# A graph network's node products, each block's transpose moved between the second and third product of the block before

## The chip, the core and the metric

The kernel runs on one core of one Trainium2 chip. The metric is the device time of one execution in microseconds (us); lower is better. Five engines work side by side on the core[...]: TensorE (PE: matrix products and transposes), VectorE (DVE: elementwise work, sums, statistics), ScalarE (ACT: activations and copies), GpSimd (POOL: here mainly the issue of gathers) and SyncE (SP: the issue of other transfers). PEld in the profile is TensorE's loading of a stationary operand.

## The reference

Two layers of a graph network on 10,000 nodes of 512 features, with 160,000 edges in order of their target. The first layer, cut to what matters:

```python
h = relu(layernorm(x))
h_all = einsum('nd,rdf->nrf', h, rel_W) + rel_b      # four products per node
agg = segment_mean(h_all[src, edge_type], dst)       # gathered over the edges
h1 = h @ self_W + self_b + agg                       # a fifth product per node
x1 = layer_norm(h + h1)
x = x + layer_norm(x1 + gelu(x1 @ W1 + b1) @ W2 + b2)
```

The second layer gathers and sums rows twice more, with two products per node each time. The change concerns only the first two lines and `h @ self_W`: the five 512x512 products of every node, called the node stage here.

## The kernel before

The nodes are taken in blocks of 128 (78 full blocks and one of 16 nodes), and the blocks in groups of four. For each block the node stage normalizes the rows, turns them on TensorE (a transpose is a product with the identity; four of them for 512 columns), copies the result out of PSUM with ScalarE, and multiplies it by five weights. All is float32, and each product of 128x512 shows as two instructions in the trace, so five products with four slabs of 128 each are 40 matmul instructions per block.

```python
def transposed(psum, dest, rows, r):
    p = psum.tile([P, KC, P], F32, name="pT")
    for k in range(KC):                                   # KC = 4
        nc.tensor.transpose(p[:, k, :r], rows[:, k * P:(k + 1) * P], ident[:r, :r])
    nc.scalar.copy(dest, p[:, :, :r])

def products(g):
    b0, nb, r = g
    xg = loaded.pop()
    sc = norm_scales(ap_, [xg[:r, c, :] for c in range(nb)], r, "a")
    hg = xp.tile([P, 4, D], F32, name="hg")
    for c in range(nb):
        h = hg[:r, c, :]
        nc.scalar.activation(h, xg[:r, c, :], AF.Relu, bias=sc[c][1], scale=sc[c][0])
        hT = ap_.tile([P, KC, P], F32, name="hT")
        transposed(psT, hT[:, :, :r], h, r)
        nc.vector.tensor_tensor(h, h, bself[:r], op=OP.add)
        nc.vector.tensor_tensor(xg[:r, c, :], xg[:r, c, :], ln2b[:r], op=OP.add)
        ha = ap_.tile([P, R, D], F32, name="ha")
        for j, w in enumerate([wself] + wrel):            # five products
            pm = psM.tile([P, D], F32, name="pm")
            for k in range(KC):
                nc.tensor.matmul(pm[:r], hT[:, k, :r], w[:, k, :], start=(k == 0),
                                 stop=(k == KC - 1))
            ...                                           # VectorE adds the bias out of PSUM
        nc.scalar.dma_start(hall_d[n0:n0 + r, :], ha[:r].rearrange("p r d -> p (r d)"))
        ...
        next(step, None)                                  # one step of the edge lists
    nc.sync.dma_start(rows_of(xs_d, g), hg[:r, :nb])
    nc.sync.dma_start(rows_of(xr_d, g), xg[:r, :nb])

for g, later in zip(groups, groups[1:] + [None]):
    products(g)
    if later:
        load(later)
```

The pools: `hT`, `ha`, `hg` and `xg` have two buffers each, the transpose's `pT` one bank of PSUM, the products' `pm` four banks, and the edge lists three banks.

`next(step)` carries on a second piece of work in small portions: the lists that say which rows each node gathers. They are worked out mostly on VectorE, with small products on TensorE in between: `pe<-inl,inb` (192 instructions), `pe<-win,of` (393) and `pe<-kept,beyond` (156). The order of the instructions on each engine in this stage is made by the scheduler of the language, which takes, in program order, what is ready by its own account of time; so an instruction may be issued before one that stands ahead of it in the text, but an engine then works through its queue in that fixed order.

Behind the node stage stands a branch that needs its results (whether the lists fit), and behind the branch the gathers and all that follows, in an order that is written by hand.

Of the kernel before, what the change touches and what calls it, by code (L numbers as in the profile page):

```python
# [8 lines left out]
F32 = mybir.dt.float32  # L9
# [3 lines left out]
AF = mybir.ActivationFunctionType  # L13
# [3 lines left out]
P = 128  # L17
# [4 lines left out]
def kernel(  # L22
# [33 lines left out]
    nc = tc.nc  # L56
    N, D = x.shape
# [3 lines left out]
    KC = D // P  # L61
# [10 lines left out]
    groups = [(b, min(4, full - b), P) for b in range(0, full, 4)]  # L72
# [59 lines left out]
    def rows_of(t, g):  # L132

        b, nb, r = g
        return t[b * P:b * P + nb * r, :].rearrange("(c p) d -> p c d", p=r)

    def wide(pool, row, n, name):

        t = pool.tile([P, n], F32, name=name)
        nc.sync.dma_start(t, bass.AP(tensor=row.tensor, offset=row.offset, ap=[[0, P], [1, n]]))  # L140
        return t

    def weight(pool, w, k, n, name, queue=nc.scalar):
        t = pool.tile([P, k, n], F32, name=name)
        queue.dma_start(t, w.rearrange("(k p) n -> p k n", p=P))
        return t

    def norm_scales(pool, vals, r, name):

        nb = len(vals)  # L150
        st = pool.tile([P, nb, 6], F32, name=f"st{name}")
        mv = pool.tile([P, nb, 2], F32, name=f"mv{name}")
        rs = pool.tile([P, 2, nb], F32, name=f"rs{name}")
        for c, v in enumerate(vals):
            nc.vector.bn_stats(st[:r, c, :], v)
            nc.vector.bn_aggr(mv[:r, c, :], st[:r, c, :])
        nc.scalar.activation(rs[:r, 0, :], mv[:r, :, 1], AF.Sqrt, bias=eps[:r], scale=1.0)
        nc.vector.reciprocal(rs[:r, 0, :], rs[:r, 0, :])
        nc.vector.scalar_tensor_tensor(rs[:r, 1, :], mv[:r, :, 0], -1.0, rs[:r, 0, :],
                                       op0=OP.mult, op1=OP.mult)  # L160
        return [(rs[:r, 0, c:c + 1], rs[:r, 1, c:c + 1]) for c in range(nb)]
# [7 lines that stand above are left out]
# [400 lines left out]
    def edges(ep, ep2, pse):  # L569
        found = {k: ep.tile([P, NB], F32, name=f"f_{k}")   # L570
                 for k in ["first", "deg", "from", "upto"] + [
                     f"{k}{lv}" for lv in range(NL) for k in ("sfrom", "supto", "sbase")]}
        with ExitStack() as s:
            yield from runs(s.enter_context(tc.tile_pool(name="er", bufs=1)), ep2, pse, found)
        with ExitStack() as s:
            yield from lists(s.enter_context(tc.tile_pool(name="el", bufs=1)), ep2, pse, found)


    with ExitStack() as s:
        pse = s.enter_context(tc.tile_pool(name="pse", bufs=3, space=PSUM))  # L580
        wp = s.enter_context(tc.tile_pool(name="wp", bufs=1))
        xp = s.enter_context(tc.tile_pool(name="xp", bufs=2))
        ap_ = s.enter_context(tc.tile_pool(name="ap", bufs=2))
        psT = s.enter_context(tc.tile_pool(name="psT", bufs=1, space=PSUM))
        psM = s.enter_context(tc.tile_pool(name="psM", bufs=4, space=PSUM))

        ep = s.enter_context(tc.tile_pool(name="ep", bufs=1))
        ep2 = s.enter_context(tc.tile_pool(name="ep2", bufs=2))
        step = edges(ep, ep2, pse)
        loaded = []  # L590

        def load(g):
            b0, nb, r = g
            loaded.append(xp.tile([P, 4, D], F32, name="xg"))
            nc.sync.dma_start(loaded[-1][:r, :nb], rows_of(x, g))

        load(groups[0])
        wself = weight(wp, self_w, KC, D, "wself")
        bself = wide(wp, self_b, D, "bself")
        wrel = [weight(wp, rel_w[0], KC, D, "wrel0", nc.sync)]  # L600
        brel = wide(wp, rel_b, R * D, "brel")
        wrel += [weight(wp, rel_w[r], KC, D, f"wrel{r}", nc.sync) for r in range(1, R)]
        ln2b = wide(wp, ln2_b, D, "ln2b")

        def products(g):
            b0, nb, r = g
            xg = loaded.pop()
            sc = norm_scales(ap_, [xg[:r, c, :] for c in range(nb)], r, "a")
            hg = xp.tile([P, 4, D], F32, name="hg")
            for c in range(nb):  # L610
                h = hg[:r, c, :]
                nc.scalar.activation(h, xg[:r, c, :], AF.Relu, bias=sc[c][1], scale=sc[c][0])
                hT = ap_.tile([P, KC, P], F32, name="hT")
                transposed(psT, hT[:, :, :r], h, r)
                nc.vector.tensor_tensor(h, h, bself[:r], op=OP.add)
                nc.vector.tensor_tensor(xg[:r, c, :], xg[:r, c, :], ln2b[:r], op=OP.add)
                ha = ap_.tile([P, R, D], F32, name="ha")
                for j, w in enumerate([wself] + wrel):
                    pm = psM.tile([P, D], F32, name="pm")
                    for k in range(KC):  # L620
                        nc.tensor.matmul(pm[:r], hT[:, k, :r], w[:, k, :], start=(k == 0),  # L621
                                         stop=(k == KC - 1))
                    if j:
                        nc.vector.tensor_tensor(ha[:r, j - 1, :], pm[:r],  # L624
                                                brel[:r, (j - 1) * D:j * D], op=OP.add)
                    else:
                        nc.vector.tensor_tensor(h, pm[:r], h, op=OP.add)
                n0 = (b0 + c) * P
                nc.scalar.dma_start(hall_d[n0:n0 + r, :], ha[:r].rearrange("p r d -> p (r d)"))
                gate[:] = [ha[:, 0, :1]] if r == P else []  # L630
                if b0 + c >= 2:
                    next(step, None)
            nc.sync.dma_start(rows_of(xs_d, g), hg[:r, :nb])
            nc.sync.dma_start(rows_of(xr_d, g), xg[:r, :nb])

        for g, later in zip(groups, groups[1:] + [None]):
            products(g)
            if later:
                load(later)
        gate.clear()  # L640
        for _ in step:
            pass

    def aligned(ctxa):
# [58 lines left out]
        with ExitStack() as s:  # L703
# [209 lines left out]
            for bs in plan:  # L913
                for b in bs:
                    r = height(b)
                    if b == bs[0]:
                        before, grp = grp, Group(bs)
                    if i + 2 < len(blocks):
                        load(blocks[i + 2])
                    if i + 1 < len(blocks):  # L920
                        hot = hots(blocks[i + 1])
                    got = second()
                    pa, mine = held
                    add(b, pa, mine)
                    v = nodes[b]
                    nc.vector.scalar_tensor_tensor(v[:r], pa[:r], rdeg[:r, b:b + 1], v[:r],
                                                   op0=OP.mult, op1=OP.add)
                    first = (b, now.stats(v[:r], r))
                    part = products(queue.pop(0) if queue else [], turning)
                    next(part)  # L930
                    now.finish()
                    scaled(got, first)
                    next(part, None)
                    if i + 1 < len(blocks):
                        held = begin(blocks[i + 1], hot, table)

                    if b == bs[0] and before:
                        queue += before.parts()
                    turning = lambda g=grp, b=b, v=v: g.turn(b, v)
                    i += 1  # L940
            turning()
            queue += grp.parts()
            while queue or fed or third:
                got = second()
                part = products(queue.pop(0) if queue else [], None)
                next(part)
                now.finish()
                scaled(got, None)
                next(part, None)
# [395 lines left out]
```

## Time and profile before

| What | Value |
|---|---|
| Time, median of 3 | 6551.81 us (6546.44 to 6563.14) |
| Span of the profiled execution | 7257.0 us |
| First product of the node stage starts | 15.61 us |
| Its last products start, and last 17.35 us | 1492.65 us |
| First gather behind the branch | 1514.47 us |
| PE busy over the whole span | 5628.8 us (78%) |
| The products, L621, on four weights and on one | 1097.8 us and 297.1 us busy |
| The transposes, L167, x316 | 48.0 us busy |
| The copies out of PSUM, L168, x79 | 45.9 us busy |

A row of the timeline gives the start, the duration, the engine, the line of the kernel, the operation with output<-input and shape, the number of instructions merged into the row, and in brackets how long the engine had been idle before and what ended it. The ends of matmuls are modelled, so intervals from start to start say more of TensorE's pace than durations do. The profiled execution is longer than the timed ones; absolute times within the node stage are read from the profile.

### The profile page before, as it was taken

Reading aid. Unit: us, or ns where it says so; the run is one execution under the profiler, and the core shown is the slowest. Engines: PE = TensorE matmul, PEld = TensorE weight load, DVE = VectorE, ACT = ScalarE, POOL = GpSimd, SP = SyncE. Lnnn points to the kernel's source line nnn. Section 1 sums busy time; section 2 is a strip of 40 time slices with the busy share of each in tenths; the row PEclk is TensorE's granted clock in tenths of the full one; section 3 lists DMA queues with packets and bytes.
Section 4 is the critical chain, followed back from the end, with each engine's and each line's share of the span. In section 5 each row is a group of like instructions: output and inputs, shape, how many; then the busy total and the mean of one; then the engine's idle time right before and its main releaser. Section 6 shows DMA issues by size and latency. Waiting matters only on the chain.

```text
span 7257.0 us, 49943 instructions
## 1 busy us (share of the span) xinstructions
PE 5628.8 (78%) x14251; PEld 2540.8 (35%) x14251; DVE 3650.8 (50%) x7301; ACT 1019.6 (14%) x1667; POOL 3807.2 (52%) x3927
## 2 busy tenths in 40 slices
PE   8999999967888899888676666666666666666666
PEld 4444444423333334333333323332322232333232
DVE  6467786235666666666334333443434444444444
ACT  1000000012222333322210010101000000000000
POOL 0001110046666666665366666666656666666665
PEclk9999999988999999999888888888887888888888
DMA  4223232256777777775466667666666777776775
GB/s 168 93 105 112 95 117 88 84 178 191 215 222 223 224 231 221 213 216 182 154 206 207 204 203 210 205 205 205 205 206 209 218 210 213 221 218 213 218 223 169
DMA packets 457021, 1360.83 MB, mean 188 GB/s; under 512 B 71902, under 2 KB 71902, under 8 KB 446606
## 3 DMA queue, kind: packets, MB, share of 16 engines
q0 software_dynamic: 308768, 1008.91, 47.1%
q1 hardware_dynamic: 136174, 265.65, 10.3%
q10 hardware_dynamic: 11792, 82.97, 2.8%
q8 instruction: 114, 1.87, 0.1%
q14 instruction: 173, 1.42, 0.1%
HBM read 1150.25 MB, written 207.01 MB: 187 GB/s over the span
## 4 chain that ended last, share of the span: by engine, by line
PE 35%; issue 23%; another core or an unknown queue 17%; DVE 4%; ACT 3%; POOL 2%; DMA 1%; ACTq 0%; POOLq 0%; DVEq 0%; SPq 0%
PE pa L688 10%; PE ph L784 6%; PE pm L621 5%; PE po L795 5%; PE po L992 4%; PE po L1026 3%; DVE pa L700 2%; POOL rows L661 2%; PE pT L167 1%; ACT hTb L168 1%; ACT mTb L168 1%; ACT mb L1022 0%; DMA rows<-hall_d,row 0%; DMA rows<-h_d,row 0%
## 5 line engine op out<-in xcount | busy, mean ns | idle before, releaser
L700 DVE TENSOR_TENSOR pa<-pa,rows 128x512 f32<-128x512 f32 x2574 | 1798.5, 699 | 991.1 <-issue 676.5
L661 POOL DMA_INDIRECT rows<-h_d,row x1716 | 1668.4, 972 | 917.5 <-issue 422.8
L661 POOL DMA_INDIRECT rows<-hall_d,row x858 | 854.2, 996 | 516.7 <-issue 193.0
L688 PE MATMUL pa<-rows,hot 128*128 128x512 f32 (+1 forms) x2358 | 1082.1, 606 | 40.0 <-issue 28.0
L992 PE MATMUL po<-wns,mTb 128*128 128x512 f32 (+1 forms) x1264 | 687.2, 694 | 537.8 <-ACT mTb L168 274.5
L1026 PE MATMUL po<-wss,hTb 128*128 128x512 f32 (+1 forms) x1264 | 710.8, 715 | 507.3 <-ACT hTb L168 393.0
L621 PE MATMUL pm<-wrel,hT 128*128 128x512 f32 (+1 forms) x2528 | 1097.8, 592 | 0.0
L661 POOL DMA_INDIRECT rows<-h_d,orow x786 | 754.7, 960 | 404.3 <-issue 223.9
L784 PE MATMUL ph<-x1T,w1s 128*128 128x512 f32 (+2 forms) x1344 | 588.0, 591 | 163.0 <-issue 88.9
L621 PEld LDWEIGHTS pm<-wrel,hT 128*128 128x128 f32 (+1 forms) x2528 | 477.3, 189 | 607.6 <-issue 584.6
L688 PEld LDWEIGHTS pa<-rows,hot 128*128 128x128 f32 (+1 forms) x2358 | 454.3, 193 | 636.5 <-issue 607.8
L661 POOL DMA_INDIRECT rows<-hall_d,orow x393 | 373.2, 950 | 453.3 <-SPq L1341 327.3
L992 PEld LDWEIGHTS po<-wns,mTb 128*128 128x128 f32 (+1 forms) x1264 | 275.6, 224 | 934.5 <-issue 631.3
L795 PE MATMUL po<-w2s,hid 128*128 128x512 f32 (+1 forms) x1264 | 564.2, 598 | 33.5 <-issue 28.7
L1026 PEld LDWEIGHTS po<-wss,hTb 128*128 128x128 f32 (+1 forms) x1264 | 277.4, 231 | 888.6 <-ACT hTb L168 448.9
L688 PE MATMUL pa<-tail,hot 128*128 128x512 f32 x936 | 465.6, 615 | 69.5 <-issue 60.7
L998 DVE TENSOR_TENSOR po<-po,bss 128x512 f32<-128x512 f32 (+1 forms) x79 | 55.0, 696 | 815.9 <-remote 740.7
L494 POOL DMA_INDIRECT win<-rec_d,at x79 | 80.4, 1018 | 661.9 <-issue 568.9
L784 PEld LDWEIGHTS ph<-x1T,w1s 128*128 128x128 f32 x1344 | 258.7, 200 | 461.7 <-issue 375.1
L624 DVE TENSOR_TENSOR ha<-pm,brel 128x512 f32<-128x512 f32 (+1 forms) x316 | 217.0, 687 | 389.5 <-PE pm L621 388.9
L1002 DVE TENSOR_TENSOR ob<-po,bss 128x512 f32<-128x512 f32 (+1 forms) x79 | 54.5, 690 | 608.8 <-remote 283.1
L795 PEld LDWEIGHTS po<-w2s,hid 128*128 128x128 f32 (+1 forms) x1264 | 237.1, 190 | 318.9 <-issue 310.8
(237 smaller groups left out, 4144.6 us busy)
## 6 DMA issues: line engine op xcount, KB each, us to landing
hall_d<-ha ACTq DMA_DIRECT2D x78, 1024.0 KB
hb<-h_d SPq DMA_DIRECT2D x38, 1024.0 KB
rows<-h_d,row POOLq DMA_INDIRECT x1716
xs<-xs_d SPq DMA_DIRECT2D x39, 512.0 KB
xr<-xr_d SPq DMA_DIRECT2D x39, 512.0 KB
xn_d<-xr SPq DMA_DIRECT2D x39, 512.0 KB
h_d<-h SPq DMA_DIRECT2D x39, 512.0 KB
xg<-in_x_dram SPq DMA_DIRECT2D x19, 1024.0 KB
```

What stands on the lines that cost most here:

```text
L167: nc.tensor.transpose(p[:, k, :r], rows[:, k * P:(k + 1) * P], ident[:r, :r])
L168: nc.scalar.copy(dest, p[:, :, :r])
L494: nc.gpsimd.indirect_dma_start(out=win[:, c, :], out_offset=None, in_=rec_d, in_offset=bass.IndirectOffsetOnAxis(ap=at[:, c:c + 1], axis=0))
L621: nc.tensor.matmul(pm[:r], hT[:, k, :r], w[:, k, :], start=(k == 0), stop=(k == KC - 1))
L624: nc.vector.tensor_tensor(ha[:r, j - 1, :], pm[:r], brel[:r, (j - 1) * D:j * D], op=OP.add)
L661: nc.gpsimd.indirect_dma_start(out=t[:n], out_offset=None, in_=table, in_offset=bass.IndirectOffsetOnAxis(ap=idx, axis=0))
L688: nc.tensor.matmul(pa[:r], hot[:, t, :r], others[t], start=(t == order[0]), stop=(t == order[-1]))
L700: nc.vector.tensor_tensor(pa[:r], pa[:r], t[:r], op=OP.add)
L784: nc.tensor.matmul(ph[:, :n], w1s[:, k, f * P:(f + 1) * P], self.xT[:, k, :n], start=(k == 0), stop=(k == KC - 1))
L795: nc.tensor.matmul(po[:r], self.hid[:, f, c * r:(c + 1) * r], w2s[:, f, :], start=(f == 0), stop=(f == FC - 1))
L992: nc.tensor.matmul(po[:r], mT[:, k, :r], wns[:, k, :], start=False, stop=(k == KC - 1))
L1026: nc.tensor.matmul(po[:r], hT[:, k, :r], wss[:, k, :], start=(k == 0), stop=False)
```

## The change

The products of all groups become one run of blocks. A block's rows are no longer turned at its own beginning but in the block before it, between that block's second and third product; the scales of a group's norms are worked out at the beginning of the last block of the group before. What it is for: while ScalarE copies the transpose out of PSUM, TensorE should have products to do. Loading the next group's rows moves to the head of the group's loop in the text. The number of instructions of every kind stays the same, and so do the pools.

```diff
-        def products(g):
+        def opened(g):
             b0, nb, r = g
             xg = loaded.pop()
-            sc = norm_scales(ap_, [xg[:r, c, :] for c in range(nb)], r, "a")
-            hg = xp.tile([P, 4, D], F32, name="hg")
+            return (xg, norm_scales(ap_, [xg[:r, c, :] for c in range(nb)], r, "a"),
+                    xp.tile([P, 4, D], F32, name="hg"))
+
+        def turned(g, rows, c):
+            r = g[2]
+            xg, sc, hg = rows
+            nc.scalar.activation(hg[:r, c, :], xg[:r, c, :], AF.Relu, bias=sc[c][1],
+                                 scale=sc[c][0])
+            hT = ap_.tile([P, KC, P], F32, name="hT")
+            transposed(psT, hT[:, :, :r], hg[:r, c, :], r)
+            return hT
+
+        rows = opened(groups[0])
+        hT = turned(groups[0], rows, 0)
+        for i, g in enumerate(groups):
+            b0, nb, r = g
+            xg, _, hg = rows
+            later = groups[i + 1] if i + 1 < len(groups) else None
+            if later:
+                load(later)
             for c in range(nb):
                 h = hg[:r, c, :]
-                nc.scalar.activation(h, xg[:r, c, :], AF.Relu, bias=sc[c][1], scale=sc[c][0])
-                hT = ap_.tile([P, KC, P], F32, name="hT")
-                transposed(psT, hT[:, :, :r], h, r)
                 ...
                 for j, w in enumerate([wself] + wrel):
+                    if j == 0 and c == nb - 1 and later:
+                        rows = opened(later)
+                    if j == 2 and c < nb - 1:
+                        hT_next = turned(g, rows, c + 1)
+                    elif j == 2 and later:
+                        hT_next = turned(later, rows, 0)
                     pm = psM.tile([P, D], F32, name="pm")
                     ...
+                hT = hT_next
...
-        for g, later in zip(groups, groups[1:] + [None]):
-            products(g)
-            if later:
-                load(later)
```

## The prediction

> **What bounds the kernel now.** I began with the slices of the page, to find the node stage and what limits it.
>
> ```profile
> PE   8999999967888899888676666666666666666666
> POOL 0001110046666666665366666666656666666665
> PEclk9999999988999999999888888888887888888888
> ```
>
> A slice is 181 us. In the first eight PE is at 9 while POOL does next to nothing; then the gathers begin and PE is no longer full. So the node stage is TensorE's, at full clock, and lasts about 1,500 us. Next, what happens at its end (POOL's timeline):
>
> ```profile
> 1514.47 0.94 POOL L661 DMA_INDIRECT rows<-hall_d,orow  x1 [327.26 <-SPq L1341]
> ```
>
> GpSimd has waited 327 us at the branch. Nothing behind the branch starts before the stage is over, so what the stage loses or gains goes into the total one for one. That carries the prediction: I need only the stage's change in microseconds. The chain of waits over the stage shows which engine sets it:
>
> ```profile
> 1269.96 17.43 PE pm L621 x40
> 1287.92 0.60 ACT hT L168
> 1288.56 17.43 PE pm L621 x40
> ...
> 1492.65 17.35 PE pm L621 x40
> 1510.03 0.69 DVE ha L624
> 1510.74 2.56 DMA hall_d<-ha
> ```
>
> Block after block: 40 products, then ScalarE's copy of the next transpose, then 40 products. PE's timeline of one such block, without edge work:
>
> ```profile
> 1287.23 0.60 PE L167 MATMUL pT<-ident,hg 128*128 128x128 f32 x4
> 1288.56 3.70 PE L621 MATMUL pm<-wself,hT 128*128 128x512 f32 x8 [0.73 <-ACT hT L168]
> 1292.10 13.90 PE L621 MATMUL pm<-wrel,hT 128*128 128x512 f32 x32
> 1305.83 0.60 PE L167 MATMUL pT<-ident,hg 128*128 128x128 f32 x4
> ```
>
> Start to start: a period of 18.60 us (1287.23 to 1305.83). The four transposes and the wait for the copy take 1.33, the first eight products 3.54, the other 32 take 13.73, so 0.429 each. At that pace the first eight would take 3.43; the wait costs 0.11 more there. The same place with edge work:
>
> ```profile
> 552.19 0.60 PE L167 MATMUL pT<-ident,hg 128*128 128x128 f32 x4
> 552.63 0.53 PE L519 MATMUL pe<-win,of 128*128 128x82 bf16 x10
> 553.00 0.32 PE L548 MATMUL pe<-kept,beyond 128*128 128x82 bf16 x4
> 553.52 3.70 PE L621 MATMUL pm<-wself,hT 128*128 128x512 f32 x8 [0.21 <-ACT hT L168]
> ```
>
> The transposes take 0.44 to the next start. Then the edge products run inside the wait for the copy (0.21 idle is left of 0.73), and from 552.19 to 553.52 is again 1.33. So the small edge products are free today: they fill the very gap that the change closes.
>
> [...] the load for a transpose stands at 1286.80, before the products are through, while behind the wait two loads come bunched, which is my reading of the 0.11. [...] The gaps here are 1.33 at most in the steady run, and the granted clock reads 1.00, so closing them wins no clock. [...] Here 32 products of 592 ns each would be 18.9 us and take 13.73, so I count starts. [...]
>
> **The change part by part.**
>
> *Transposes between the second and third product.* A block now is 40 products at 0.429, 17.16 us, plus the transposes, 0.44, plus what the switch to them and back costs. The way there costs nothing visible (their start follows at the products' pace); the way back I put at 0.1 us, an estimate from the 0.11 that bunched weight loads cost above. Sum 17.70 against 18.60: 0.90 saved. There are 78 passages from one block to the next: 0.90 x 78 = 70 us.
>
> *The edge products lose their hiding place.* 393 of `pe<-win,of` and 156 of `pe<-kept,beyond`; ten of them took 0.37 from 552.63 to 553.00, 0.037 each: 549 x 0.037 = 20 us, now on TensorE's path wherever the scheduler puts them. The 192 of `pe<-inl,inb` were never hidden (a period with 32 of them, from 318.82 to 340.86, is 22.04, longer by 3.44): no change.
>
> *The second block.* It starts at 37.40 after a wait of 2.44 instead of 0.73, since the first group's start ran into ScalarE's other work. With its transpose seven microseconds into block one that goes: 1.7 us saved.
>
> *Norms a block ahead, loads at the head of the loop.* Already today the scheduler runs them early: the relus of four blocks stand together at 1222.69, and the next group starts at 1232.81. In the text they move, in time hardly. 0.
>
> *Evictions and stores.* Same number, same place; VectorE takes 0.69 per product of 3.43 and `pm` has four banks. 0.
>
> Sum: 70 + 1.7 - 20 = 52 us. I take off 7 for stalls: today two edge products waited 2.50 and 3.18 us for VectorE with the queue behind them, and smaller lateness was swallowed by the gap, which it won't be any more. 45 us remain, and the stage ends near 1465 instead of 1510: 6551.8 - 45 = 6507 us, 0.7% less.
>
> **The rivals.**
>
> *VectorE takes over in the list stretch.* For it (the window from 850 to 1000 us; columns are PE, PEld, DVE, ACT and POOL busy, granted clock, DMA share, GB/s):
>
> ```profile
> 850.00:1000.00 150.00, 145.64 (x461) 68.15 (x460) 123.41 (x535) 11.14 (x18) 16.27 (x16) 0.99 0.27 101
> ```
>
> VectorE is busy 82% here. With 70 - 20 us off some 1,480 the share rises to about 85%: still below TensorE, but more edge products would come late. The lists occupy about 750 us, some 40 blocks. If a third of those blocks met a stall of 2.5 us, that took 33 us, and the gain shrank to about 20: 6532. Against it: only two such stalls today, and they depend on the scheduler's order more than on load.
>
> *The copy is held up on ScalarE.* Its queue can stand at relus that wait for a store:
>
> ```profile
> 1222.69 2.93 ACT L612 ACTIVATE hg<-xg,rsa 128x512 f32<-128x512 f32 x4 [8.79 <-DMA xs_d<-hg]
> ```
>
> That block began at 1213.96. If the next block's copy stands behind these relus, it starts 11.7 us into the block and is done by 12.3, and is needed at 17.7. Slack of five microseconds; cost nothing. If such a pile-up came later in the block, at 20 group ends, 20 x 2 = 40 us would be lost: 6545, no change.
>
> *The edge products stay hidden.* They might fill bubbles at the switch back to products. Then 20 us come on top: gain 70, 6482. I see no gap of that size in a queue that always has products ready, so I give it little.
>
> *Nothing comes through, because the branch waits for something else.* The lists end at about 1250 us, 260 before the stage does, so only the last block's products and its store of 2.56 us stand before the gathers. Against this rival.
>
> **Range and chances.** The working gives 6507. The largest doubts are the way back from the transposes (0 to 0.25 us each, +8 to -12 us in all) and stalls of edge products (0 to 30 us); the times of before spread over 17 us. I say 6488 to 6533 for 8 in 10. Two per cent is 131 us; the waits to be had are 1.33 + 0.11 - 0.44 = 1.0 us in 78 passages, 78 us, so faster by 2% can't come from this mechanism: 0.02. Slower by 2% would need 1.7 us lost at every block, or a bad order: 0.02. Within 2%: 0.96.
>
> **What would show it.** Right: in blocks without edge work a period of about 17.7 us, with 16 products, four transposes, 24 products; the wait of PE for the copy (30.5 us in 67 cases today) gone; edge products adding some 0.5 us to a block that has them; the first gather near 1470. Wrong: idle time of PE before `pe` products with VectorE as releaser, well above 5.7 us; a bubble of over 0.25 us behind the transposes; PE waiting for the copy or for relus in mid-block; or a granted clock under 1.00 in the stage.

## The result, and the profile after

| | Before | After |
|---|---|---|
| Time, median | 6553.04 us (4 runs) | 6504.61 us (4 runs, 6497.32 to 6506.94) |
| Ratio to before | | 0.9923, 95% interval 0.9906 to 0.9940 |
| First gather behind the branch | 1514.47 us | 1461.25 us |
| PE waits for the copy, `pm <- hT` | 30.5 us, 67 times | 0.7 us, once |
| PE waits for VectorE before `pe` products | 3.2, 2.5 and 0.4 us | none |

The kernel is 48 us faster, 0.8%; run again beside other kernels it came to 6496.57 us, ratio 0.9919 (0.9906 to 0.9933). The profiled execution of the kernel before ran slower behind the branch than its timed ones, so traces are compared up to the first gather only.

The slices of the page after (40 equal parts of the span, each digit a share in tenths):

```profile
PE   9999999996999999999877777777778777777777
POOL 0001111007777777777277777777767777777776
PEclk9999999998999999999998889888888998888988
```

A slice is 163 us now; the stage fills the first nine, at a granted clock of 1.00 (the window from 20.5 to 1460.8 us). POOL's timeline at the branch:

```profile
1461.25 0.95 POOL L681 DMA_INDIRECT rows<-hall_d,orow  x1 [313.11 <-SPq L1361]
```

The gathers still wait for the stage, and begin 53.2 us earlier. The chain of waits of this profile covers only the last instructions of the execution, so what sets the stage is read from PE's timeline. A block without edge work:

```profile
1252.43 0.60 PE L167 MATMUL pT<-ident,hg 128*128 128x128 f32 x4
1252.87 10.46 PE L645 MATMUL pm<-wrel,hT 128*128 128x512 f32 x24
1263.17 3.60 PE L645 MATMUL pm<-wself,hT 128*128 128x512 f32 x8
1266.60 3.60 PE L645 MATMUL pm<-wrel,hT 128*128 128x512 f32 x8
1270.03 0.60 PE L167 MATMUL pT<-ident,hg 128*128 128x128 f32 x4
```

No brackets: nothing was waited for. Transposes to transposes is 17.60 us, against 18.60. The transposes take 0.44, and the 24 products behind them 10.30, which is 24 times the usual 0.429: coming back to products costs nothing. A block with edge work:

```profile
507.62 10.46 PE L645 MATMUL pm<-wrel,hT 128*128 128x512 f32 x24
517.92 0.53 PE L519 MATMUL pe<-win,of 128*128 128x82 bf16 x10
518.29 0.32 PE L548 MATMUL pe<-kept,beyond 128*128 128x82 bf16 x4
518.45 3.67 PE L645 MATMUL pm<-wself,hT 128*128 128x512 f32 x8
521.95 1.45 PE L645 MATMUL pm<-wrel,hT 128*128 128x512 f32 x3
```

The edge products stand between two blocks and take their full 0.53 us, and the eight products behind them 3.50 instead of 3.43. (The last row is cut off by the window of the view; the next product of the block begins at 521.95.) And the list stretch, the window from 850 to 1000 us (columns: length, then busy time of PE, PEld, DVE, ACT and POOL, granted clock, DMA share, GB/s):

```profile
850.00:1000.00 150.00, 150.00 (x478) 70.02 (x477) 123.60 (x547) 11.72 (x19) 16.43 (x16) 1.00 0.29 106
```

TensorE has no idle time at all in it; VectorE is as busy as before.

### The profile page after: what moved, and what is told of

It is laid out like the page before. It is cut to its first block, busy times and chain, and to the rows that moved or that the text cites. A ratio compares the mean times of both kernels' runs of the same rounds, so it can differ in the third digit from the quotient of the medians.

```text
span 6504.3 us, 49918 instructions
## 1 busy us (share of the span) xinstructions
PE 5603.6 (86%) x14251; PEld 2472.9 (38%) x14251; DVE 3632.4 (56%) x7301; ACT 1013.0 (16%) x1667; POOL 3823.7 (59%) x3927
## 5 line engine op out<-in xcount | busy, mean ns | idle before, releaser
L708 PE MATMUL pa<-rows,hot 128*128 128x512 f32 (+1 forms) x2358 | 1364.7, 718 | 673.8 <-DMA rows<-h_d,orow 615.9
L708 PEld LDWEIGHTS pa<-rows,hot 128*128 128x128 f32 (+1 forms) x2358 | 492.8, 225 | 1537.7 <-DMA rows<-h_d,orow 1078.5
L681 POOL DMA_INDIRECT rows<-h_d,orow x786 | 786.5, 1001 | 355.7 <-issue 129.0
L1012 PE MATMUL po<-wns,mTb 128*128 128x512 f32 (+1 forms) x1264 | 572.7, 596 | 1.5 <-ACT mTb L168 1.5
L1046 PE MATMUL po<-wss,hTb 128*128 128x512 f32 (+1 forms) x1264 | 572.3, 596 | 0.0
L804 PE MATMUL ph<-x1T,w1s 128*128 128x512 f32 (+2 forms) x1344 | 557.9, 568 | 4.8 <-ACT hid L806 4.8
L1042 ACT ACTIVATE mb<-pa,rdeg 128x512 f32<-128x512 f32 (+1 forms) x158 | 108.5, 687 | 1835.0 <-DVE pa L720 1825.9
L1012 PEld LDWEIGHTS po<-wns,mTb 128*128 128x128 f32 (+1 forms) x1264 | 239.9, 190 | 307.9 <-issue 305.7
L1046 PEld LDWEIGHTS po<-wss,hTb 128*128 128x128 f32 (+1 forms) x1264 | 228.6, 191 | 232.0 <-issue 232.0
L645 PE MATMUL pm<-wself,hT 128*128 128x512 f32 (+1 forms) x632 | 290.3, 602 | 0.7 <-ACT hT L168 0.7
```

The costliest lines, as they stand in the source:

```text
L681: nc.gpsimd.indirect_dma_start(out=t[:n], out_offset=None, in_=table, in_offset=bass.IndirectOffsetOnAxis(ap=idx, axis=0))
L708: nc.tensor.matmul(pa[:r], hot[:, t, :r], others[t], start=(t == order[0]), stop=(t == order[-1]))
L804: nc.tensor.matmul(ph[:, :n], w1s[:, k, f * P:(f + 1) * P], self.xT[:, k, :n], start=(k == 0), stop=(k == KC - 1))
L1012: nc.tensor.matmul(po[:r], mT[:, k, :r], wns[:, k, :], start=False, stop=(k == KC - 1))
L1042: nc.scalar.activation(m[:r], pa[:r], AF.Copy, scale=rdeg[:r, b:b + 1])
L1046: nc.tensor.matmul(po[:r], hT[:, k, :r], wss[:, k, :], start=(k == 0), stop=False)
```

## Experiments

"First gather" is when GpSimd begins behind the branch, from the profile. It repeats well: 1461.25 us in the kernel after, 1461.26 in its second run. The ratio is to the kernel before on the same chip.

| Kernel | First gather | Time, median | Ratio (95% interval) |
|---|---|---|---|
| before | 1514.47 | 6553.04 | |
| after; again | 1461.25; 1461.26 | 6504.61; 6496.57 | 0.9923; 0.9919 (0.9906 to 0.9933) |
| e1_end | 1504.20 | 6544.54 | 0.9985 (0.9977 to 0.9994) |
| e9_behind_lists | 1513.01 | 6556.01 | 0.9997 (0.9989 to 1.0005) |
| e2_fifth | 1461.28 | 6497.42 | 0.9919 (0.9904 to 0.9934) |
| e5_one_hT | 1508.69 | 6549.33 | 0.9992 (0.9986 to 0.9999) |
| e6_inside | 1472.01 | 6512.67 | 0.9937 (0.9923 to 0.9950) |
| e3_twice_after | 1475.20 | 6515.62 | 0.9941 (0.9927 to 0.9954) |
| e4_twice_before | 1588.92 | 6622.18 | 1.0102 (1.0087 to 1.0118) |
| e8_twice_end | 1506.30 | 6544.69 | 0.9984 (0.9977 to 0.9990) |
| e11_twice_behind | 1581.09 | 6630.08 | 1.0104 (1.0087 to 1.0121) |
| e10_small_start | 1458.41 | 6498.66 | 0.9913 (0.9899 to 0.9926) |

**Turned at the block's end.** In the kernel after:

```diff
                 for j, w in enumerate([wself] + wrel):
-                    if j == 2 and c < nb - 1:
-                        hT_next = turned(g, rows, c + 1)
-                    elif j == 2 and later:
-                        hT_next = turned(later, rows, 0)
                     ...
+                if c < nb - 1:
+                    hT_next = turned(g, rows, c + 1)
+                elif later:
+                    hT_next = turned(later, rows, 0)
                 hT = hT_next
                 ...
                     next(step, None)                      # the step of the edge lists
```

> Everything of the change stays (one run of blocks, norms a block ahead, loads at the head), but a block's rows are turned behind the fifth product of its predecessor instead of between the second and third. My theory (the position of the transposes is all of the gain): TensorE waits for the copy again, the period without edge work is 18.6 us, the first gather is at 1512 to 1516 us, the total at 6545 to 6560 us. The rival (norms and loads ahead bring the gain): the first gather stays near 1461 us, the total near 6505 us.

PE's timeline:

```profile
1258.35 0.60 PE L167 MATMUL pT<-ident,hg 128*128 128x128 f32 x4
1259.68 3.70 PE L641 MATMUL pm<-wself,hT 128*128 128x512 f32 x8 [0.73 <-ACT hT L168]
1263.22 13.90 PE L641 MATMUL pm<-wrel,hT 128*128 128x512 f32 x32
```

The wait of 0.73 is back and the period is 18.60, as my theory had it; the rival falls. But the first gather comes at 1504.2 and not at 1512 to 1516: 10 us of the 53 stay. Position is 43 us; something else is the rest. Block by block the two kernels differ most at two places, where the kernel before does this:

```profile
942.60 0.78 PE L548 MATMUL pe<-kept,beyond 128*128 128x82 bf16 x16
943.22 0.62 PE L167 MATMUL pT<-ident,hg 128*128 128x128 f32 x4
943.68 0.53 PE L519 MATMUL pe<-win,of 128*128 128x82 bf16 x10
946.71 0.36 PE L519 MATMUL pe<-win,of 128*128 128x82 bf16 x5 [2.50 <-DVE of L445]
946.91 5.37 PE L621 MATMUL pm<-wself,hT 128*128 128x512 f32 x8
```

Sixteen edge products stand before the transposes and fifteen behind them, and the last five are not fed yet: the queue stands for 2.50 us, with the products behind it ready. ScalarE's copy for them was through at 945.02 us, and they begin at 946.91, behind the last edge product. The eight products behind the stall then take 5.20 us (946.91 to the next row at 952.11), where they take 3.51 behind a stall in e9_behind_lists below; the last section says why. Around the two stalls four periods are longer by 9.7 us in all, 1.0 of which are the two batches of sixteen themselves. In this experiment TensorE has no wait for VectorE in the whole stage.

**Turned behind the step of the edge lists.** As above, with the four new lines and `hT = hT_next` behind `next(step, None)`, the order in the text that the kernel before has. What is left of the change is the one run of blocks, norms ahead and loads ahead.

> Transposing at the block's end was 10 us faster at the first gather (1504.2 us) than the kernel before (1514.5 us), though its period was the same 18.6 us. Here the transposes move once more, behind the block's step of the edge lists, where the kernel before has them; norms and loads stay ahead. Theory A (what made the 10 us is the rank of the transposes before the edge products, which then lie in the wait for the copy): first gather 1511 to 1517 us, total near 6553 us. Theory B (it is the norms a block ahead, which no longer crowd VectorE): first gather near 1504 us, total near 6544 us.

PE's waits (us in total, times, longest):

```profile
PE pm L641 <- ACT hT L168: 30.2, 67, 2.2
...
PE pe L519 <- DVE both L467: 2.6, 1, 2.6
PE pe L519 <- DVE of L445: 2.5, 1, 2.5
```

The two stalls are back, at 1513.0 us, and the time can't be told from that of the kernel before. So theory A: norms and loads ahead bring nothing that can be told apart, and the rank of the transposes before the list step brings 8.8 us (1513.01 to 1504.20). Added up by periods, 6.9 of these are the two stalls and 4.2 the `pe<-inl,inb` products, more of which lie in the wait for the copy; some 2 are lost again at the second block of e1_end.

**Turned between the fourth and the fifth product**, `j == 4` for `j == 2` twice.

> The transposes stand between the fourth and the fifth product of the block before. From their start to the next block's first product there are then 0.44 + 3.43 us; the chain of transposes and copy took 1.33 us in the kernel before. My theory: that is enough, the period stays 17.6 us, the first gather at 1459 to 1464 us, the total at 6495 to 6515 us. The rival (the copy needs the long distance, because ScalarE may stand at relus that wait for a store): waits of some microseconds at group ends, up to 20 x 2 = 40 us more, 6545 us.

First gather 1461.28 us. One product of 3.43 us in between is as good as three, and the waits that the rival needs do not occur. In the kernel after, the pile-up of relus I had feared stands behind the copy, not before it (ScalarE's timeline):

```profile
1253.12 0.58 ACT L168 COPY hT<-pT 128x512 f32<-128x512 f32 x1 [17.02 <-PE pT L167]
1254.16 2.93 ACT L616 ACTIVATE hg<-xg,rsa 128x512 f32<-128x512 f32 x4 [0.45 <-DMA xs_d<-hg]
```

**One buffer for the turned block.**

```diff
-            hT = ap_.tile([P, KC, P], F32, name="hT")
+            hT = ap_.tile([P, KC, P], F32, name="hT", bufs=1)
```

> The kernel after with one buffer instead of two for the turned block. TensorE's order is that of the kernel after in the blocks without edge work; only the copy has to wait until the last product of the block before has read the buffer. My theory (what is gained is the copy beside the products, not the place of the transposes as such): per block 17.17 for the products, 0.44 for the transposes, 0.9 for the copy with its semaphores, 0.1 for the first weight loads, 18.6 in all as in the kernel before, with the edge products hidden in that wait again; first gather 1508 to 1518 us, total 6545 to 6560 us. The rival (an early transpose is enough by itself): near 6505 us.

```profile
1252.27 0.60 PE L167 MATMUL pT<-ident,hg 128*128 128x128 f32 x4
1252.70 10.47 PE L645 MATMUL pm<-wrel,hT 128*128 128x512 f32 x24
1263.90 3.70 PE L645 MATMUL pm<-wself,hT 128*128 128x512 f32 x8 [0.73 <-ACT hT L168]
```

The transposes stand where the change put them, and the wait of 0.73 has only moved behind the 24 products. Nearly the whole gain is gone (6549.33 us). The change lives on the second buffer, which the kernel before had and could not use.

**Ahead within groups only.** The line `elif j == 2 and later` goes; the next group's first block is turned behind the last product of the group.

> Blocks are turned ahead within a group of four only; the first block of a group is turned behind the last product of the group before. My theory: the gain is additive by passages, 20 of 78 passages fall back to 18.6 us, which is 1.0 us each, less some 0.4 us of edge products hidden again at about ten of them: first gather 1475 to 1480 us, total 6513 to 6527 us. The rival (groups were the obstacle: most of the gain comes from running over the group's border): more than half of the gain goes, total over 6530 us.

10.8 us of the 43 go, about a quarter, for 20 of the 78 passages; so the gain adds up by passages and the rival falls. The first gather, 1472.0 us, is 3 us below my range. A border without edge work costs 1.0 us (two blocks take 36.21 us instead of 35.21), but in the list stretch only 0.55 per group (73.06 for four blocks against 72.50), because edge products hide in the wait again.

**Edge products twice, after and before.** In either kernel:

```diff
-                    nc.tensor.matmul(pm[:, t, :], of[:, t * P:(t + 1) * P], ...)
+                    for again in range(2):
+                        nc.tensor.matmul(pm[:, t, :], of[:, t * P:(t + 1) * P], ...)
```

> The kernel after with each of the 393 edge products of 128x82 in bf16 issued twice (the second writes the same result). My theory (with the gap closed they lie on TensorE's path at full price): 393 x 0.037 = 14.5 us more, the first gather at 1474 to 1478 us, the total at 6513 to 6525 us. The rival (they still run in bubbles): 6500 to 6510 us, first gather near 1461 us.

> The same doubling in the kernel before. There the wait for the copy leaves 0.89 us behind the transposes, of which 0.37 to 0.52 are filled; 0.37 more still fit. My theory: at most 3 us more, first gather 1513 to 1518 us, total 6548 to 6560 us. The rival (edge products cost the same in both kernels): 14.5 us more, first gather 1529 us, total near 6567 us.

> The kernel after itself, beside the two doublings. First gather at 1460 to 1463 us, total at 6497 to 6510 us by either theory; it shows how far the time of the stages behind the branch varies by itself.

After: 13.9 us more (1475.20 against 1461.26), 0.0355 for each of the 393. Full price, as expected. Before: 74.5 us more, where I had said 3 and the rival 14.5. Neither theory held. The waits of PE there:

```profile
PE pe L520 <- DVE both L467: 37.2, 13, 3.4
PE pm L622 <- ACT hT L168: 26.1, 50, 1.9
...
PE pe L549 <- DVE both L467: 7.6, 4, 1.9
PE pe L520 <- DVE of L445: 2.0, 4, 0.5
```

46.8 us of waiting for VectorE in place of 5.7, and behind such stalls 14 stretches at half clock in place of two (last section). The room in the gap was counted rightly, as the next pair shows, and was not what mattered.

**Edge products twice, with the transposes before and behind the list step**: the same edit in e1_end and in e9_behind_lists.

> Doubling the edge products cost 14.0 us at the first gather in the kernel after and 74 us in the kernel before, with waits of TensorE for VectorE of 47 us. Here the same doubling in the kernel that transposes at the block's end. Theory A (a gap in front of the products draws more edge products into the queue than VectorE can feed, and they hold up the products): waits of PE for VectorE of 30 us or more, 40 to 75 us more than without the doubling, total 6585 to 6620 us. Theory B (norms at the head of the group made the crowd, and they are ahead here): at most 5 us more, total near 6547 us.

> The doubled edge products in the kernel that turns a block behind the step of the edge lists, with norms and loads still ahead. Doubling cost 74 us in the kernel before and 2 us with the transposes in front of the step. Theory A (the rank of the transposes before or behind the list step decides whether edge products are queued that VectorE has not fed yet): first gather 1570 to 1600 us, waits of PE for VectorE over 35 us, total 6605 to 6635 us. Theory B (norms a block ahead are what takes the stalls away): first gather near 1515 us, hardly any such waits, total near 6557 us.

Before the step, 2.1 us more (1504.20 to 1506.30) and not one wait for VectorE: nineteen edge products fit into the wait for the copy.

```profile
624.94 0.60 PE L167 MATMUL pT<-ident,hg 128*128 128x128 f32 x4
625.38 0.86 PE L520 MATMUL pe<-win,of 128*128 128x82 bf16 x19
626.27 3.70 PE L642 MATMUL pm<-wself,hT 128*128 128x512 f32 x8
```

Behind the step, 68.1 us more (1513.01 to 1581.09), with waits for VectorE of 46.1 us:

```profile
608.94 0.53 PE L520 MATMUL pe<-win,of 128*128 128x82 bf16 x10
609.31 0.32 PE L549 MATMUL pe<-kept,beyond 128*128 128x82 bf16 x4
609.46 0.62 PE L167 MATMUL pT<-ident,hg 128*128 128x128 f32 x4
609.92 0.53 PE L520 MATMUL pe<-win,of 128*128 128x82 bf16 x10
613.30 0.55 PE L520 MATMUL pe<-win,of 128*128 128x82 bf16 x6 [2.85 <-DVE both L467]
613.65 5.23 PE L642 MATMUL pm<-wself,hT 128*128 128x512 f32 x8
```

A batch of edge products goes ahead of the transposes, and behind them stands part of the next batch, which VectorE has not fed. Theory A of e8_twice_end, that a gap draws in such products by itself, fell: the gap is there in both. What differs is the transposes' place, and behind the list step the stalls come. Whether the gap is needed for them too is open, since no run has that place without a gap. That the scheduler's account of time differs from the chip's may be the reason why such a product is queued at all; that was not tried.

**A first group of one block.**

```diff
-    groups = [(b, min(4, full - b), P) for b in range(0, full, 4)]
+    groups = [(0, 1, P)] + [(b, min(4, full - b), P) for b in range(1, full, 4)]
```

> The kernel after with a first group of one block, then groups of four: the first transfer is a quarter as long, and one block's norms instead of four stand before the first transpose (it starts at 14.1 us now, the statistics of the other three blocks take some 2 us of that). If the start waits for these, the first gather comes 3 to 5 us earlier (1457 us) and the total falls by as much; if it waits for the weights, which are on their way at the same time, nothing changes (1461 us).

The first product starts at 8.59 us instead of 15.90, but the second group's rows are late then (TensorE waits 1.44 us for its relu, and the second block starts 23.02 after the first). First gather 2.8 us earlier; in the total it can't be told from the kernel after.

## Why the prediction was right, and where its terms were off

The forecast was 6507 us, the measured time 6504.61. The mechanism was the one foretold: TensorE sets the stage, the stage passes its gain on (in every row of the table of experiments the total moved against the kernel before as the first gather did, within 6 us), the copy runs beside products, and edge products pay for it. That the total came within 3 us is in part luck: the first gather moved by 53 us and not by 45, and the repeated run gained 57 us in the total. Step by step, in microseconds of first gather:

| Step of the prediction | Foretold | Shown |
|---|---|---|
| 78 passages, the period of a plain block | 18.60 to 17.70, 70 | 18.60 to 17.60, 78 |
| Edge products of 128x82 lose their hiding place | -20 | -24 |
| The 192 of `pe<-inl,inb`, "no change" | 0 | about -8, and -2 for other small products there |
| The second block's start | +1.7 | about +1 |
| Norms and loads ahead | 0 | 0 to 1.5 |
| Stalls of edge products | -7 | +9.7 |
| Sum | 45 | 53.2 |

The shown terms are rounded sums over periods and add up to within 3 us.

*The way back from the transposes*, put at 0.1 us, costs nothing (24 products in 10.30 us). In the trace the load stands ahead of its start at the switch both ways: the transposes' first load at 1252.00 and their start at 1252.43, the products' at 1252.76 and 1252.87. Two loads come bunched at 1252.76 as well, and nothing is lost; so the bunching in which I had read the 0.11 is not what costs it. The starts behind a wait show it (1263.90 to 1267.44 in e5_one_hT, 3.54 us for eight products).

*Edge products*: two blocks with 24 of them last 36.25 us (18.21 + 18.04) against 35.21 without, 1.04 more, over some 20 such pairs, and 0.7 more for each of the five batches of sixteen. I had counted the products and not the 0.07 that each return from them costs.

*"Never hidden"* was read from one period of 22.04, where 32 of these products stand before the transposes. Others had stood in the gap, for instance eight at 148.01 us, with a period of 18.6 as if they were not there. Added up against the base period, the stretch from 230 to 450 us carried 14.2 us in the kernel before and 23.9 after; of these the 192 products are 13 and 21. One block of a kind was taken for all.

*Stalls* had the wrong sign, and this is the step that failed. I took the two stalls of 2.50 and 3.18 us as bound to stay and expected more. They went, because the transposes got out of the way of the list step: e1_end is without them, e9_behind_lists has them. With the slow products behind them and their batches they had cost 9.7 us. The working also took the clock as 1.00 in the whole stage; two stretches of 3.41 us at 0.50 lay in it behind these stalls, about 1.7 us lost in each, and went with them. This term and the one above nearly cancel, so that by luck the sum came out closer than its parts.

The rivals: VectorE stayed as busy as before, with no stall. The copy was not held up on ScalarE, and even one product of distance was enough. Edge products hiding elsewhere is refuted by the full 13.9 us of their doubling in the kernel after. That nothing comes through is refuted by 1461.25.

## What to carry to other kernels

Here the copy between two uses of TensorE was hidden by giving TensorE one later product to do, not by an early start as such: it took the second buffer on the copy's output (with one buffer the first gather came at 1508.69 us, with two at 1461.25), and one product of 3.43 us was distance enough for a chain of 1.33 (less was not tried). Before closing a gap, count what else runs in it over the whole stage, not in one block: here some 34 us of other products came back onto the path. And where a scheduler interleaves a second stream in an engine that works through its queue in order, as TensorE did at the 2.50 us above, the rank of the dependent link before that stream is a change by itself: with the gap still open, 9 us here, and 75 with the second stream's products doubled (1581.09 against 1506.30).

## What the runs showed of the hardware that was not expected

In these runs a stall of TensorE cost more than its idle time in some cases. Behind the stall of 2.50 us in the kernel before, eight products took 5.20 us; in e9_behind_lists the same eight took 3.51 behind a stall of 2.45. The difference is the granted clock (the view by windows, columns as above):

```profile
947.10:950.50 3.40, 3.40 (x5) 1.34 (x5) 3.40 (x23) 0.00 (x0) 0.00 (x0) 0.50 0.08 34
```

In this stretch products start 0.853 us apart instead of 0.429. The kernel before has a second one from 1100.7 us, also at 0.50; the kernel after has none in its stage.

Which pause was followed by such a stretch went with how it fell in time. In the clock records of all thirteen traces, up to 1440 us, every change lies on a grid of 3.41 us that has its own phase in each execution. In 31 windows of this grid that half clock followed, TensorE was busy for 0.23 to 1.57 us (0.91 and 0.23 in the kernel before); in the other 5,300 or so at full clock it was busy for 1.53 us or more. So in the kernel before the pause at the second block (transposes from 34.37, products from 37.40) fell across two windows with 2.68 and 1.71 us of work, and the eight products behind it took 3.54. In e1_end the pause at the same place (35.81 to 38.56) fell into one window with 1.27 us of work, and they took 5.23. So half clock came behind windows with as much as 1.57 us of work too, counted with modelled ends of products. Why it does was not shown.
